# A Fourier-operator tokenizer with transformer: the mixing of modes without GpSimd and in a fixed order, its weights in eighths, its modes loaded in two parts

## The chip, the cores and the metric

One core of a Trainium2 chip. The metric is device time in microseconds (us). Engines are named as in the profile: PE multiplies matrices (PEld loads its weights), DVE, ACT and POOL (GpSimd) are the vector, scalar and general engines, SP only issues DMAs. A "q" behind a name (SPq, ACTq) is the engine's queue of DMA issues.

## What is computed

64 images of 256 x 256 pass a four-layer Fourier neural operator with 32 channels; its output, one value a pixel, is 256 rows of 256 values. With 77 text rows these are 333 tokens of 256, which pass one transformer layer (attention, and a feed-forward part for the 165 kept tokens). Cut to the part around the change:

```python
v = h @ p_w + p_b                                   # 3 -> 32 channels
for i in range(4):
    x_ft = rfft2(v)                                 # 24 x 12 modes are kept
    out_ft[:12, :12]  = einsum('bixy,ioxy->boxy', x_ft[:, :, :12, :12],  W1[i])
    out_ft[-12:, :12] = einsum('bixy,ioxy->boxy', x_ft[:, :, -12:, :12], W2[i])
    v = irfft2(out_ft) + einsum('bcxy,cd->bdxy', v, w_w[i]) + w_b[i]
    v = batchnorm(v)                                # over all images and pixels
    if i < 3: v = relu(v)
out = einsum('bcxy,cu->bxyu', v, q_w) + q_b         # then attention and feed-forward
```

All of it is in float32. The batch norm needs sums over all images before any pixel of the next layer can be made; the kernel takes them in the space of modes.

## The kernel before, in words

For each of the four layers there is a **mixing**, and after each of the first three a **pass** over the 64 images. The fourth mixing is followed by the transformer (`image_rows` to `feed_forward`).

A pass (`layer`) reads an image's pixels (tile vin, L578), makes the new pixels (`pre`: L614 from the mixed modes, L625 from the old pixels), applies ReLU into vo (L632 on ACT, L633 on DVE), stores vo (L634 on SP), transposes it into t32 (L637), squares a product for the variance (`product`, L649 and L656), and transforms the new pixels to modes: `along_y` (L666, four t32 tiles of an image, result zt by L676) and `along_x` (L689), whose 72 KB for one image (xo) are stored to xh_d in HBM (L697). `load_am` (L564) loads the mixed modes of an image, `scale_am` (L584, POOL) scales them into one of two tiles ams, `spread` (L595) is the first matmul with them. The pass is written in a region with manual schedule: each engine keeps the order in which the code is written. All else is ordered by the framework's scheduler, which simulates the program and issues what is ready by the order of writing.

A mixing has these steps. `mix_weights` makes the tiles wm of the two halves of mode rows from the weights in HBM: `piece(m)`, four pieces, loads 2.36 MB into a tile wn by four DMAs (L361; on SP in layer 0, on POOL in the others), then copies into wm (L376 and L378 on ACT, L380 on DVE); the first piece of a half also fills two slots on POOL (L366, L367). There is one wn tile in layer 0 and two in the others. L746 loads the modes of all 64 images, 4.7 MB, into the tile xh (in layer 0 `forward_first` makes them on the chip, with 12 additions at L302). `squares` sums the squares of the pass. `mix` then has 12 steps kp: 96 small matmuls (L412), an eviction into e by ACT (L424), four copies into the output tiles ob (L429 and L432 on DVE, L430 on POOL, L431 on ACT), two instructions and a product for the sums (L434, L438 or L440), their addition into acc (L441, POOL), copies for the edges (L442, L449), and four stores of 256 KB to mix_d (L451). There are three ob tiles of each part. After the 12 steps come the statistics (L458 to L486). `layer` begins with the constant rows of the two ams tiles: a memset (L536) and small DMAs on ACT's queue (L544), 28 in layer 0 and 4 in layers 1 and 2, and in layer 0 with two loads of 2 MB into the tiles mv (L557).

The pools of tiles are stacks of SBUF addresses: the pools of a pass lie where those of a mixing lay before, and the other way round. With `reuse_waits="tile"` a new tile waits only for the earlier tiles whose bytes it takes. In order of address, behind the constants (offsets in bytes of one partition, from the sizes in the code):

| | mixing, layers 1 to 3 | pass before |
|---|---|---|
| | wn 0, xh 36864, wm 73728 to 129024 | li (vin, mv) 0, lc (ams, sk) 32768, lt (t32) 39552, ly (y_) 121472, lo (vo) 137856, lz (zt) 170624, lx (xo) 178816, la (am) 179968 |

Of the kernel before, what the change touches and what calls it, by code (L numbers as in the profile page):

```python
# [9 lines left out]
F32 = mybir.dt.float32  # L10
# [7 lines left out]
C = 32  # L18
# [16 lines left out]
def _tables():  # L35
# [10 lines left out]
    def halves(a):  # L46
        return a.reshape(2, 128, -1).transpose(1, 0, 2)
# [34 lines left out]
    out["ones"] = np.ones((128, 128))  # L82
    out["chan"] = p[:, None] % C == np.arange(C)[None, :]

    out["fyr"] = halves(fy)
    out["fyi"] = halves(np.concatenate([np.sin(th), np.cos(th), np.zeros((S, 8))], 1))
    out["fxn"] = halves(np.concatenate([cs, grid[:, None], np.zeros((S, 15))], 1))
# [42 lines left out]
def tile_fno_fusion_transformer(ctx: ExitStack, tc: tile.TileContext, a, cst_d, grid_d, out):  # L130
# [14 lines left out]
        nc.sync.dma_start(t, cst_d[:, lo:hi])  # L145
        return lambda k: t[:, _AT[k][0] - lo:_AT[k][0] - lo + _AT[k][1]]

    tab = tables(const, "fyt", "chan", "cst")
    FYT = tab("fyt").rearrange("p (y k) -> p y k", y=8)
    EXL = {n: tab("ex" + n) for n in "EO"}  # L150
    FXL = {n: tab("fx" + n).rearrange("p (h k) -> p h k", h=2) for n in "EO"}
    T4, ID, ONES, CHAN = tab("t4"), tab("ident"), tab("ones"), tab("chan")

    epsc = const.tile([128, 1], F32, name="epsc")
    nc.vector.memset(epsc, EPS)
# [33 lines left out]
    def forward_first(xh, weights):  # L189
# [4 lines left out]
        with tc.tile_pool(name="f0", bufs=1) as fp, tc.tile_pool(name="f0i", bufs=3) as ip, \  # L194
# [42 lines left out]
                    )  # L237

            weights(0)

            pw, pb = a["L0_tok_p_w"], a["L0_tok_p_b"].rearrange("(o c) -> o c", o=1)
            pwR = fp.tile([128, C], F32, name="pwR")
# [48 lines left out]
            for kyg in range(3):  # L291
                for ri in range(2):
                    t2 = [pq.tile([128, 2, 512], F32, name="xps") for _ in range(2)]
                    for j in range(4):
                        nc.tensor.matmul(
                            t2[j // 2][:, j % 2, :kn * B],
                            lhsT=px[32 * j:32 * j + KX, kyg, ri].rearrange("p q c -> p (q c)"),
                            rhs=xm[32 * j:32 * j + KX], start=True, stop=True, skip_group_check=True,
                        )
                    for j in range(2):  # L300
                        k0 = 2 * kn * j
                        nc.vector.tensor_tensor(  # L302
                            xh[:, kyg, ri, k0:k0 + 2 * kn, :].rearrange("p (j k) b -> p j k b", j=2),
                            t2[j][:, :, :kn * B].rearrange("p j (k b) -> p j k b", b=B),
                            g[:, kyg, ri, k0:k0 + 2 * kn, :].rearrange("p (j k) o -> p j k o", j=2)
                            .to_broadcast([128, 2, kn, B]),
                            ALU.add,
                        )
                if kyg < 2:
                    weights(kyg + 1)  # L310
            weights(3)


            mo = fp.tile([128, 4], F32, name="mo")
# [34 lines left out]
    def mix_weights(i, wmp, wnp):  # L349

        wms = [wmp.tile([128, 3, M, 6, C], F32, name=f"wm{half}") for half in range(2)]

        def piece(m):
            half, oh = divmod(m, 2)
            wm, fw = wms[half], a[f"L0_tok_fw{half + 1}"]
            n = 16 * M * M * 2
            wn = wnp.tile([128, n], F32, name="wn")
            for k4 in range(4):  # L360
                (nc.gpsimd if i else nc.sync).dma_start(  # L361
                    wn[C * k4:C * k4 + C, 0:n - 2 * k4],
                    fw[i, :, 16 * oh:16 * oh + 16].rearrange("c o k l r -> c (o k l r)")[:, 2 * k4:],
                )
            if oh == 0:
                nc.gpsimd.memset(wm[:, :, :, 5, :], 0.0)  # L366
                nc.gpsimd.tensor_copy(  # L367
                    wm[:, :, :, 2, :].rearrange("p g k o -> p (g k) o"),
                    w4[i].rearrange("p (o c) -> p o c", o=1).to_broadcast([128, 3 * M, C]),
                )  # L370
            v = wn.rearrange("p (o k g q r) -> p g k o q r", o=16, k=M, g=3, q=4)
            for slot, ri in ((4, 1), (3, 0), (1, 0), (0, 1)):
                s_ = v[:, :, :, :, 0, ri]
                d_ = wm[:, :, :, slot, 16 * oh:16 * oh + 16]
                if slot == 0:
                    nc.scalar.mul(d_, s_, -1.0)  # L376
                elif slot == 1:
                    nc.scalar.copy(d_, s_)  # L378
                else:
                    nc.vector.tensor_copy(d_, s_)  # L380

        return wms, piece

    def mix(i, lhs, wm, u2):
# [5 lines left out]
        with tc.tile_pool(name="mo", bufs=1) as op, tc.tile_pool(name="me", bufs=3) as ep, \  # L390
                tc.tile_pool(name="mp", bufs=2, space=PSUM) as pp:
            NB = 3
            ob = [[op.tile([128, C, 32], F32, name=f"ob{p}_{n}") for n in range(NB)] for p in range(2)]
            for p in range(2):
                for n in range(NB):
                    nc.gpsimd.memset(ob[p][n], 0.0)
            acc = op.tile([128, 12, 2, C], F32, name="acc")
            f0 = op.tile([128, M, 2, C], F32, name="f0")
            fr = op.tile([128, M, 2, C], F32, name="fr")
# [3 lines left out]
            for kp in range(M):  # L403
                ps = pp.tile([128, 4, 512], F32, name="mps")
                wk, k0 = wm[2 * kp // M], 2 * kp % M
                for g in range(3):
# [11 lines left out]
                e = ep.tile([128, 3, 4, 4, C], F32, name="e")  # L418
                a_ = ep.tile([128, 12, 2, C], F32, name="a_")
                o0, o1 = (  # L420
                    ob[p][kp % NB][:, :, :KX].rearrange("p o (n k) -> p n k o", k=M) for p in range(2)
                )
                for hv in halves:
                    nc.scalar.copy(  # L424
                        e[hv].rearrange("p g q s o -> p q g (s o)"),
                        ps[hv, :, 0:384].rearrange("p q (g s) -> p q g s", g=3),
                    )
                    ev = e[hv].rearrange("p g q s o -> p (g q) s o")
                    nc.vector.tensor_copy(o0[hv, 0], ev[:, :, 1, :])  # L429
                    nc.gpsimd.tensor_copy(o0[hv, 1], ev[:, :, 2, :])  # L430
                    nc.scalar.mul(o1[hv, 0], ev[:, :, 2, :], -1.0)  # L431
                    nc.vector.tensor_copy(o1[hv, 1], ev[:, :, 1, :])  # L432
                    for n, (us, fs) in enumerate(((0, 1), (3, 2))):
                        nc.vector.scalar_tensor_tensor(  # L434
                            a_[hv, :, n, :], ev[:, :, us, :], 2.0, ev[:, :, fs, :], ALU.mult, ALU.add
                        )
                    if kp == 0:
                        nc.vector.tensor_mul(acc[hv], a_[hv], ev[:, :, 1:3, :])  # L438
                    else:
                        nc.vector.tensor_mul(a_[hv], a_[hv], ev[:, :, 1:3, :])  # L440
                        nc.gpsimd.tensor_add(acc[hv], acc[hv], a_[hv])  # L441
                    nc.scalar.copy(f0[hv, kp], ev[:, 0, 1:3, :])  # L442
                if kp == 0:
                    nc.vector.tensor_add(fin[0:B, 1, :], e[0:B, 0, 0, 1, :], e[0:B, 0, 0, 0, :])
                for kk in range(2):
                    to = (M - kp) % M if kk == 0 else M - 1 - kp
                    hv = slice(64 * kk, 64 * kk + B)
                    if kk or kp != M // 2:
                        nc.scalar.copy(fr[hv, to], e[hv, 0, 0, 1:3, :])  # L449
                    for p in range(2):  # L450
                        nc.sync.dma_start(  # L451
                            mix_d[i][:, p, 2 * kp + kk, :], ob[p][kp % NB][hv].rearrange("b o k -> b (o k)")
                        )
            for hv in halves:
                q = fin[hv, 0, :]
                t1 = op.tile([128, C], F32, name="t1", bufs=2)
# [45 lines left out]
    def layer(i, st, src, dst, acc):  # L502
# [7 lines left out]
        with ExitStack() as cx:  # L510
            def pool(name, bufs, **kw):
                return cx.enter_context(tc.tile_pool(name=name, bufs=bufs, **kw))

            ip = pool("li", 2 if i == 0 else 4, reuse_waits="tile")
            cp = pool("lc", 1, reuse_waits="tile")
            tp, yp, op, zp, xp = (
                pool(n, k, reuse_waits="tile") for n, k in (("lt", 5), ("ly", 2), ("lo", 4), ("lz", 1), ("lx", 2))
            )
            ap_ = pool("la", 2, reuse_waits="tile")
            pp = pool("lp", 4, space=PSUM)  # L520


            rv = cp.tile([128, 4, C], F32, name="rv")

            ams = [cp.tile([64 + rows_, 16 * C], F32, name=f"ams{n}") for n in range(2)]
            if i == 0:
                nc.vector.tensor_mul(rv[:, 0, :], s_, w0row[:, 3, :])
                nc.vector.tensor_add(rv[:, 0, :], rv[:, 0, :], t_)
# [3 lines left out]
            else:  # L532
                nc.vector.tensor_copy(rv[:, 0, :], t_)
            nc.vector.tensor_scalar_mul(rv[:, 0, :], rv[:, 0, :], float(S * S))
            for t in ams:
                nc.vector.memset(t, 0.0)  # L536
                av = t.rearrange("p (c k) -> p c k", k=32)
                halves = [(n, 64 * n, slice(16 * n, 16 * n + 16)) for n in range(2)]
                where = [(0, 48, 0)]
                if i == 0:  # L540
                    where += [(1, 48, 28), (2, 49, 0)] + [(3, 50 + j, 24 + j) for j in range(4)]
                for n, r, k in where:
                    for _, p0, cs in halves:
                        nc.scalar.dma_start(av[p0 + r:p0 + r + 1, :, k], rv[0:1, n, cs])  # L544
            sk = cp.tile([128, 16, 32], F32, name="sk")
            for _, p0, cs in halves:
                nc.vector.tensor_copy(
# [183 lines left out]
    st = None  # L731
    acc = None
    for i in range(L):
        with tc.tile_pool(name="wn", bufs=2 if i else 1, reuse_waits="tile") as wnp, \
                tc.tile_pool(name="xh", bufs=1, reuse_waits="tile") as xp, \
                tc.tile_pool(name="wm", bufs=1, reuse_waits="tile") as wmp:
            wm, piece = mix_weights(i, wmp, wnp)
# [3 lines left out]
                lhs = lambda band, g, ri, k: xh[band, g, ri, k, :]  # L741
            else:
                xh = xp.tile([128, B, 3, 2, KX], F32, name="xh")
                piece(0)
                piece(1)
                nc.sync.dma_start(xh.rearrange("p b g r k -> p b (g r k)"), xh_d[i - 1])  # L746
                u2 = squares(i, acc)
                piece(2)
                piece(3)
                lhs = lambda band, g, ri, k: xh[band, :, g, ri, k]  # L750
            st = mix(i, lhs, wm, u2)
        if i < L - 1:
            acc = const.tile([128, 16 * B], F32, name="acc") if acc is None else acc
            with tc.manual_schedule():
# [375 lines left out]
```

## Time and profile before

| | us |
|---|---|
| median of 3 runs | 12465.9 (12437.0 to 12485.34) |
| the profiled execution | 12478.4, span 12476.6 |
| PE busy | 11172.7 (90% of the span) |
| DVE, ACT, POOL busy | 8784.2, 6065.1, 1529.5 |
| mean clock granted to PE | 0.957 |
| from the first weight load of a mixing to the first matmul after it | 59.3 to 248.2; 3106.1 to 3257.1; 6403.0 to 6554.6; 9691.9 to 9857.9 |

In the lines below a row of a timeline has the start in us, the duration in us, the engine, the line of the code, the operation, output<-input with partitions x elements, how many instructions are merged, and in brackets how long the engine had stood still and what ended that. A row of windows has the window and its length, then for PE, PEld, DVE, ACT and POOL the busy us (and the number of instructions), then the granted clock (1.00 is full), the mean share in which the 16 DMA engines were busy, and GB/s.

### The profile page before, as it was taken

To read this page: it belongs to the slowest core of one execution; us is meant where nothing else is said; L and a number is where in the kernel's file an instruction comes from. 1 tells how busy PE (TensorE), PEld (TensorE's weight loads), DVE (VectorE), ACT (ScalarE), POOL (GpSimd) and SP (SyncE) were. 2 spreads that over 40 slices of the span, in tenths; PEclk is the share of its full clock that TensorE was granted. 3 is DMA by queue.
4 is the path that set the end of the run, shared out by engine and by line. 5 is a ranking of instruction groups with operands and counts; after the bars stand their busy time and mean duration, and the time that the engine had idled before them with its cause. 6 is when DMAs were issued, how large, how long until landed. Compare 5 with 4: busy or idle time off the path is not lost. (4 is left out here: it accounts for less than half of the span.)

```text
span 12476.6 us, 405217 instructions
## 1 busy us (share of the span) xinstructions
PE 11172.7 (90%) x182038; PEld 5874.2 (47%) x182038; DVE 8784.2 (70%) x10531; ACT 6065.1 (49%) x10217; POOL 1529.5 (12%) x2040
## 2 busy tenths in 40 slices
PE   4999999999699999999969999999999599999999
PEld 2444444444344444444434444444444366666666
DVE  4777777777677777777767776777777566666665
ACT  4555555555455555555545555555555333333333
POOL 1000000000100000000010000000000233333333
PEclk7999999999799999999989999999999799999999
DMA  6555555555899899889889898899899755555553
GB/s 187 199 202 202 201 202 202 200 201 203 286 350 350 346 351 353 344 345 349 341 277 358 345 354 347 341 351 352 345 352 352 255 218 229 232 227 221 221 231 151
DMA packets 588469, 3485.04 MB, mean 279 GB/s; under 512 B 96616, under 2 KB 146152, under 8 KB 189800
## 3 DMA queue, kind: packets, MB, share of 16 engines
q1 hardware_dynamic: 540288, 3405.18, 70.9%
q0 software_dynamic: 38144, 50.22, 1.8%
q8 instruction: 1423, 23.31, 0.7%
q10 hardware_dynamic: 8296, 3.72, 0.1%
q14 instruction: 318, 2.61, 0.1%
HBM read 1761.83 MB, written 1696.92 MB: 277 GB/s over the span
## 5 line engine op out<-in xcount | busy, mean ns | idle before, releaser
L656 ACT ACTIVATE ring<-ring 128x1024 f32<-128x1024 f32 x3072 | 3108.8, 1012 | 1185.5 <-PE ring L649 1148.6
L637 DVE STREAM_TRANSPOSE t<-vo 128x2048 f32<-128x2048 f32 x1536 | 3550.1, 2311 | 175.2 <-ACT vo L632 13.5
L649 PE MATMUL ring<-vo,w 32*32 32x512 f32 x49152 | 2851.0, 625 | 385.4 <-DVE zt L676 134.1
L632 ACT ACTIVATE vo<-ring 128x1024 f32<-128x1024 f32 x1536 | 1568.1, 1021 | 3045.8 <-PE ring L625 2386.1
L633 DVE TENSOR_SCALAR vo<-ring 128x1024 f32<-128x1024 f32 x1536 | 1858.6, 1210 | 615.0 <-PE ring L625 420.5
L666 PE MATMUL ring<-t,cst 32*32 32x512 f32 x49152 | 1867.6, 603 | 297.8 <-issue 296.6
L676 DVE STREAM_TRANSPOSE zt<-ring 128x1024 f32<-128x1024 f32 x384 | 712.3, 1926 | 1646.6 <-PE ring L666 1646.6
L649 PEld LDWEIGHTS ring<-vo,w 32*32 32x32 f32 x49152 | 765.5, 105 | 1886.4 <-ACT ring L656 473.7
L584 POOL TENSOR_TENSOR ams<-am,sk 48x512 f32<-48x512 f32 x384 | 486.7, 1268 | 8538.7 <-DMA am<-mix 8218.2
L666 PEld LDWEIGHTS ring<-t,cst 32*32 32x32 f32 x49152 | 976.3, 103 | 1145.6 <-issue 688.7
L625 PE MATMUL ring<-vin,ws 32*32 32x512 f32 x32768 | 1241.9, 607 | 21.2 <-issue 19.2
L689 PEld LDWEIGHTS ring<-cst,zt 128*128 128x128 f32 x4608 | 536.1, 194 | 179.4 <-ACT vo L632 159.5
L1079 POOL DMA_DIRECT2D out_dram<-o x1024 | 512.3, 509 | 660.1 <-DVE o L1074 628.8
L656 ACT ACTIVATION_READ_ACCUMULATOR ring<-ring 128x1 f32 x3072 | 584.2, 190 | 0.0
L689 PE MATMUL ring<-cst,zt 128*128 128x96 f32 x4608 | 568.3, 280 | 8.3 <-DVE zt L676 8.3
L878 PE MATMUL hp<-ch,win 128*32 128x512 f32 x4096 | 473.3, 602 | 8.6 <-DMA ch<-v 8.5
L595 PE MATMUL ring<-ams,cst 49*128 49x512 f32 (+1 forms) x1536 | 391.5, 620 | 99.4 <-POOL ams L584 88.7
L625 PEld LDWEIGHTS ring<-vin,ws 32*32 32x32 f32 x32768 | 253.8, 103 | 410.0 <-issue 382.8
L883 ACT ACTIVATE h<-hp,hbias 128x512 f32<-128x512 f32 x64 | 44.0, 687 | 597.5 <-PE hp L878 581.4
L412 PE MATMUL mps<-wm,xh 32*64 32x128 f32 (+1 forms) x4608 | 110.4, 354 | 242.2 <-DMA xh<-xh 110.8
L595 PEld LDWEIGHTS ring<-ams,cst 49*128 49x128 f32 (+1 forms) x1536 | 147.5, 188 | 349.8 <-issue 242.1
L1041 PE MATMUL pp<-zs,w 128*128 128x165 f32 x2048 | 302.4, 305 | 0.0
(932 smaller groups left out, 12039.4 us busy)
## 6 DMA issues: line engine op xcount, KB each, us to landing
v<-vo SPq DMA_DIRECT2D x1536, 1024.0 KB
vin<-v SPq DMA_DIRECT2D x1024, 1024.0 KB
ch<-v SPq DMA_DIRECT2D x512, 1024.0 KB
mix<-ob SPq DMA_DIRECT2D x192, 256.0 KB
am<-mix SPq DMA_DIRECT2D x384, 96.0 KB
xin<-in_x_dram SPq DMA_DIRECT2D x16, 1024.0 KB
mv<-in_x_dram SPq DMA_DIRECT2D x256, 64.0 KB
out_dram<-o POOLq DMA_DIRECT2D x1024, 16.0 KB, 3.0
```

The costliest lines, as they stand in the source:

```text
L584: nc.gpsimd.tensor_tensor(ams[b % 2][hv], a_[hv], sk[hv].rearrange("p c k -> p (c k)"), ALU.mult)
L595: nc.tensor.matmul(ps[:, n, :], lhsT=EX[hv, 128 * h:128 * h + 128], rhs=ams[b % 2][hv], start=True, stop=True, skip_group_check=True,)
L625: nc.tensor.matmul(ps[n][32 * j:32 * j + 32], lhsT=ws[32 * n:32 * n + 32], rhs=v[32 * n:32 * n + 32, 2 * j:2 * j + 2, :], start=False, sto ...
L632: nc.scalar.activation(of[:, 0:2], t2[0], AF.Relu)
L633: nc.vector.tensor_scalar(of[:, 2:4], t2[1], 0.0, None, ALU.max)
L637: nc.vector.transpose(t32[b, t // 2][:, :, 8 * (t % 2):8 * (t % 2) + 8, :].rearrange("p y s c -> p s y c"), o.rearrange("p s (y l) -> p s ...
L649: nc.tensor.matmul(ps[n][32 * j:32 * j + 32], lhsT=w4[i + 1][32 * n:32 * n + 32], rhs=o[32 * n:32 * n + 32, 2 * j:2 * j + 2, :], start=Tru ...
L656: nc.scalar.activation(t2[n], t2[n], AF.Square, accum_out=acc[:, at:at + 1])
L666: nc.tensor.matmul(ps[n][32 * j:32 * j + 32], lhsT=FYT[32 * n:32 * n + 32, k, :], rhs=t32[b, j][32 * n:32 * n + 32, k].rearrange("p s c -> ...
L676: nc.vector.transpose(zt[:, h].rearrange("p k c -> p c k"), t2[h].rearrange("p n (s c) -> p c (n s)", c=C),)
L689: nc.tensor.matmul(ps[:, 0, 96 * g:96 * g + 96], lhsT=zt[:, h, k0:k0 + 4, :].rearrange("p k c -> p (k c)"), rhs=FX[:, h, 48 * r:48 * r + 9 ...
L1079: nc.gpsimd.dma_start(out[b, 64 * n + 16 * g:64 * n + 16 * g + 16].rearrange("(p t) d -> p t d", t=2), o[32 * g + 8 * n:32 * g + 8 * n + 8 ...
```

## The change

1. Weights come in eight pieces of half the size, with two wn tiles in layer 0 and four in the others. In layer 0 two pieces are asked for before the parameters, the others two by two after each group of modes.
2. In layers 1 to 3 the modes are loaded in two parts: those of the first 56 images on POOL's queue, written after the first four pieces, those of the last eight on SP.
3. `mix` is put into a region with manual schedule. In it POOL's copy and addition go to DVE, one DVE copy goes to ACT and one ACT copy (f0) to DVE, and the copies into ob are written before the sums. The two parts of ob lie in one tile, so that a step has two stores of 512 KB.
4. The constant rows of ams come from a table of zeros and ones (64 KB more in the table of constants), multiplied by the row's values on DVE, without DMAs.
5. The pools of a pass have another order: lo 32768, ly 65536, la 81920, lc 86016, lx 93056, lz 94208, lt 102400 to 184320 (in bytes behind the constants, as above).

```diff
@@ forward_first
             weights(0)
+            weights(1)
...
-                if kyg < 2:
-                    weights(kyg + 1)
-            weights(3)
+                weights(2 * kyg + 2)
+                weights(2 * kyg + 3)
@@ mix_weights
-            half, oh = divmod(m, 2)
+            half, oh = divmod(m, 4)
...
-            n = 16 * M * M * 2
+            n = 8 * M * M * 2
@@ mix
-            ob = [[op.tile([128, C, 32], F32, name=f"ob{p}_{n}") for n in range(NB)] for p in range(2)]
-            for p in range(2):
-                for n in range(NB):
-                    nc.gpsimd.memset(ob[p][n], 0.0)
+            ob = [op.tile([128, 2, C, 32], F32, name=f"ob{n}") for n in range(NB)]
+            for t in ob:
+                nc.gpsimd.memset(t, 0.0)
...
+                    nc.scalar.mul(o1[hv, 0], ev[:, :, 2, :], -1.0)
+                    nc.scalar.copy(o1[hv, 1], ev[:, :, 1, :])
                     nc.vector.tensor_copy(o0[hv, 0], ev[:, :, 1, :])
-                    nc.gpsimd.tensor_copy(o0[hv, 1], ev[:, :, 2, :])
-                    nc.scalar.mul(o1[hv, 0], ev[:, :, 2, :], -1.0)
-                    nc.vector.tensor_copy(o1[hv, 1], ev[:, :, 1, :])
+                    nc.vector.tensor_copy(o0[hv, 1], ev[:, :, 2, :])
+                    nc.vector.tensor_copy(f0[hv, kp], ev[:, 0, 1:3, :])
...
-                        nc.gpsimd.tensor_add(acc[hv], acc[hv], a_[hv])
-                    nc.scalar.copy(f0[hv, kp], ev[:, 0, 1:3, :])
+                        nc.vector.tensor_add(acc[hv], acc[hv], a_[hv])
...
-                    for p in range(2):
-                        nc.sync.dma_start(
-                            mix_d[i][:, p, 2 * kp + kk, :], ob[p][kp % NB][hv].rearrange("b o k -> b (o k)")
-                        )
+                    nc.sync.dma_start(
+                        mix_d[i][:, :, 2 * kp + kk, :], ob[kp % NB][hv].rearrange("b p o k -> b p (o k)")
+                    )
@@ layer
-            for t in ams:
-                nc.vector.memset(t, 0.0)
...
-                        nc.scalar.dma_start(av[p0 + r:p0 + r + 1, :, k], rv[0:1, n, cs])
...
+            for n in range(nr):
+                nc.vector.tensor_tensor(
+                    a1 if n else a0, rh[:, n].to_broadcast([128, 16, 32]),
+                    CROW[:, n:n + 1, :].to_broadcast([128, 16, 32]), ALU.mult,
+                )
+                if n:
+                    nc.vector.tensor_add(a0, a0, a1)
+            nc.vector.tensor_copy(ams[1], ams[0])
@@ the loop over the layers
-        with tc.tile_pool(name="wn", bufs=2 if i else 1, reuse_waits="tile") as wnp, \
+        with tc.tile_pool(name="wn", bufs=4 if i else 2, reuse_waits="tile") as wnp, \
...
-                piece(0)
-                piece(1)
-                nc.sync.dma_start(xh.rearrange("p b g r k -> p b (g r k)"), xh_d[i - 1])
+                early = max(B - 8, 0)
+                for m in range(4):
+                    piece(m)
+                if early:
+                    nc.gpsimd.dma_start(
+                        xh[:, :early].rearrange("p b g r k -> p b (g r k)"), xh_d[i - 1][:, :early]
+                    )
+                nc.sync.dma_start(
+                    xh[:, early:].rearrange("p b g r k -> p b (g r k)"), xh_d[i - 1][:, early:]
+                )
                 u2 = squares(i, acc)
-                piece(2)
-                piece(3)
+                for m in range(4, 8):
+                    piece(m)
...
-            st = mix(i, lhs, wm, u2)
+            with tc.manual_schedule():
+                st = mix(i, lhs, wm, u2)
```

## The prediction

> **What bounds the kernel now.** I first read the page's rows of 40 slices: PE is at 9 tenths nearly everywhere, with a dip at each of the four mixings. Inside the passes (3300 to 6300 us) PE is busy 2771 of 3000 us and the clock granted is 0.99; the change touches nothing there. So I read the four gaps, from the first weight load of a mixing to the first matmul after it: 59.3 to 248.2 us (layer 0), 3106.1 to 3257.1, 6403.0 to 6554.6, and 9691.9 to 9857.9. The middle two are alike. The view of windows for the second (span, then PE, PEld, DVE, ACT, POOL, clock, DMA share, GB/s):
>
> ```profile
> 3106.00:3152.00 46.00, 19.25 (x346) 11.08 (x342) 14.91 (x14) 10.86 (x16) 17.68 (x26) 0.72 1.01 241
> 3152.00:3166.00 14.00, 0.00 (x0) 0.00 (x0) 0.00 (x0) 0.00 (x0) 0.00 (x0) 0.50 0.97 354
> 3166.00:3188.00 22.00, 10.65 (x480) 9.92 (x480) 15.25 (x20) 13.74 (x20) 7.39 (x5) 0.73 0.02 6
> 3188.00:3224.00 36.00, 17.44 (x672) 15.81 (x672) 32.78 (x37) 21.45 (x38) 20.79 (x14) 0.55 0.90 243
> 3224.00:3244.00 20.00, 0.66 (x2) 0.50 (x2) 16.18 (x37) 3.69 (x8) 5.32 (x5) 0.50 0.37 84
> ```
>
> The DMA engines are full until 3166, then empty for 22 us, full again, and mostly empty for 20 us before the end. No compute engine is full throughout. The timeline of SP's queue and then of PE says why:
>
> ```profile
> 3130.73 0.32 SPq L697 DMA_DIRECT2D xh<-xo  x1
> 3145.97 0.32 SPq L746 DMA_DIRECT2D xh<-xh  x1
> 3187.51 63.10 SPq L451 DMA_DIRECT2D mix<-ob  x48
> 3253.61 0.79 SPq L564 DMA_DIRECT2D am<-mix  x2
> ```
>
> ```profile
> 3168.52 7.59 PE L412 MATMUL mps<-wm,xh 32*64 32x128 f32 x326 [37.36 <-DMA xh<-xh]
> ...
> 3257.13 5.11 PE L595 MATMUL ring<-ams,cst 49*128 49x512 f32 x8 [21.07 <-POOL ams L584]
> ```
>
> The one load of all modes (L746) stands until the pass's last 72 KB store (L697) has landed, 14.8 us by SP's waits, and the mixing until that load has landed. Its first store leaves only at 3187.5, since the scheduler put the copies into ob behind the sums and the weights of the second half. The last stores leave after the statistics, and the load of am waits for them. DVE's timeline shows the second fault:
>
> ```profile
> 3177.58 2.67 DVE L434 SCALAR_TENSOR_TENSOR a__30837<-e 128x384 f32<-128x384 f32 x2
> ...
> 3186.57 0.48 DVE L429 COPY ob<-e 128x384 f32<-128x384 f32 x1
> ...
> 3188.96 1.03 DVE L434 SCALAR_TENSOR_TENSOR a__30904<-e 128x384 f32<-128x384 f32 x2 [0.93 <-ACT e L424]
> ...
> 3195.16 2.12 DVE L432 COPY ob<-e 128x384 f32<-128x384 f32 x1
> ```
>
> The same pair of L434 takes 1.03 us while POOL is idle and 2.67 while POOL adds (L441 at 3177.75); a copy 0.48 or 2.12. Layer 0, by windows and by ACT's timeline:
>
> ```profile
> 76.00:100.00 24.00, 13.40 (x66) 7.47 (x62) 17.77 (x38) 2.71 (x3) 4.72 (x6) 0.62 0.05 12
> 100.00:112.00 12.00, 0.00 (x0) 0.00 (x0) 0.16 (x1) 0.18 (x1) 0.69 (x1) 0.50 0.83 173
> ...
> 200.00:230.00 30.00, 0.66 (x2) 0.50 (x2) 6.45 (x29) 2.02 (x3) 0.00 (x0) 0.50 0.43 96
> 230.00:248.00 18.00, 0.00 (x0) 0.00 (x0) 0.00 (x0) 0.00 (x0) 1.09 (x1) 0.50 0.73 255
> ```
>
> ```profile
> 206.22 6.92 ACTq L544 DMA_DIRECT2D ams<-rv  x11
> 213.18 0.85 ACT L431 ACTIVATE ob<-e 128x384 f32<-128x384 f32 x1 [6.13 <-DMA ams<-rv]
> 213.21 13.54 ACTq L544 DMA_DIRECT2D ams<-rv  x16
> ```
>
> With one weight buffer the DMA engines stand idle from 76 to 100, and 28 tiny DMAs on ACT's queue hold up the last copies into ob, behind them the last stores, the 4 MB of mv and am.
>
> **The floor.** I price a gap by what the DMA engines must move, as they are its fullest resource. Weights: 9.43 MB, queue q0 used 21.2% of 195 us in the window 3085 to 3280, so 41.3 us. Modes: 4.72 MB at 354/0.97 = 365 GB/s, 12.9. Stores of mix: 12.58 MB at 243/0.90 = 270 GB/s, 46.6. The pass's last v stores: some 4. Sum 105 us from 3106.1, so 3211; the ends (last store to am to POOL to PE, 3250.3 to 3257.1) add 6.8: 3218, against 3257.1. So 39 us of this gap are DMA idleness.
>
> **The change, part by part, in gaps 2 and 3.**
> *Modes of 56 images early.* By the order of the pools the modes' tile now lies on the vo tiles and one y_ tile, free after the last transpose and store of vo, about 3112, no longer on t32 (free after along_y, 3122). 4.13 MB move under along_y and along_x; 0.59 MB stay behind L697. The load goes to POOL's queue, in order behind 16 weight issues of 0.49 us; it adds one issue. The price of the new places: wm's first half now lies on xo and zt, so its copies wait until the last xo store lands. Before, they ran at 3122.4. I keep 14.8 us for that store (3145.5), and five us of copies after it: the first matmul at about 3152, not 3168.5. Behind that wait stand POOL's memset and copy (2.2 us) and, if the scheduler puts them first, POOL's later loads, so between 3135 (store lands at once) and 3158 (early load behind the memset); I take 3152.
> *Weights in eighths.* Same bytes. 32 issues for 16, 7.8 us more on POOL, hidden as POOL has no arithmetic left. 16 more copies, each with a fixed 0.19 us by ACT's rows (64 elements 0.24, 1536 1.44): 1.6 us on ACT and on DVE, inside the coupling below. But pieces 4 to 7 can load only after pieces 0 to 3 are copied, now about 3149: some 20 us of DMA that lay before 3152 move beside the stores. The sum of bytes holds that already.
> *No GpSimd, fixed order.* DVE per step: two copies 0.49, the f0 copy about 0.15 (nearest row L442 on ACT, 0.25), the pair 1.03, product 0.96, the add that was L441 0.96 (row L440): 4.1 us, 49 for 12, plus 4.6 for the weights' copies. ACT: 1.44 + 0.88 + 0.88 + 0.49 = 3.7. POOL's 1.1 and 1.8 us and their slowing of DVE go. PE's 96 matmuls take 2.6. Stores need 46.6/12 = 3.9 us a step. A new wait: in fixed order o1 on ACT and o0 on DVE wait until the store of three steps before has landed, and the next eviction and the sums stand behind them. First eviction 3155, so DVE is done by 3210; the statistics take 5.8 + 0.8 + 2.3 us by their rows, constants 2.7: 3222, POOL and PE 3223.
> *Constant rows.* In layers 1 and 2 four DMAs of 0.6 us on ACT go; three to four DVE instructions of 0.5 replace two memsets of 0.49: within 1 us. The table is 64 KB more at the start: 0.2 us.
> DMA path 3218, engine path 3223, nearly level. For their coupling (stores beside weights, a drained queue about 3147) I add 6: 3229. Gain **28** each.
>
> **Layer 0.** xin's rest 4, weights 9.43 MB at 173/0.83 = 208 GB/s 45.3, stores 46.6, mv 4.19 MB 10.5 (387 GB/s at share 0.97), ends 9.7: 59.3 + 116 = 175, against 248.2. Kept idle: some 12 us while the first copies of weights wait in DVE's order for the 12 adds of L302 (77.7 to 88.4), and 10 of coupling: 198. The constants cost about 5 us of DVE for 1.0 of memsets, under mv's load; without that cover 4 us. Gain **50**.
> **Layer 3.** Weights, modes, stores 100.8, v 3, the transformer's parameters 13 (ACT's queue, 7.8% of 166 us) and tables 2: 119; ends 12.9: 9824 against 9857.9. The parameter issues stay on ACT between the mixing's steps (they held L431 5.2 and 4.7 us), now in a fixed chain: I keep 14. Gain **20**.
> Sum 50 + 28 + 28 + 20 = **126 us**. The profiled execution took 12478.4 (span 12476.6): it would take 12352. The median of the three is 12.5 lower: 12340.
>
> **Two rules of the skill.** The Trainium skill, SBUF — State Buffer, section "SBUF: two separate sides", speaks against this change: descriptors of POOL's DMAs can't be written while DVE copies fp32 in SBUF, and the summary says to issue from SP or ACT. Its example goes from 620 to 3100 ns. Row: L361, 489 ns in median, 712 at most, six of 16 while DVE was busy 9.7 of 10 us (in transposes, not copies). By the row nothing; by the rule 16 pieces beside the mixing would each land up to 2.5 us late, 40 us if in series, under 22 us of loads that must run anyway: 10 to 20 a gap. I take the row and keep the rule for the range. DMA: Bandwidth & Descriptors, "Queues, rings and completion order", says that an engine takes queues in turn by packets; the 72 KB would then land in about 2 us and the start come at 3142. The row says 14.8. It is worth at most 6 us, as the stores end last.
>
> **Rivals.**
> A, chance 0.62: as worked out, 12340.
> B, 0.12: all idleness goes except layer 0's 12 us and 4 a gap: 60 + 35 + 35 + 30 = 160, 12306. For it: the slack is real; against: copies must wait for loads.
> C, 0.12: the stores starve behind the eighths as L697 did, ob's wait then stops ACT and DVE until the loads end, about 3180, and all 46.6 us follow: 3180 + 46.6 + 6.8 = 3233 plus coupling 4. Gains 33, 20, 20, 12 = 85: 12381.
> D, 0.10: the scheduler, outside the fixed part, sets loads and copies as late as before; the start stays at 3168 and only the tail's idleness goes (13 us of the 20): 35 + 14 + 14 + 7 = 70, 12396; one part of this is a change that doesn't do what it says.
> E, slower, 0.04: the pools' new order puts vin, vo and t32 elsewhere; should a pass run slower by that, in its 9.2 ms (three passes), 1.4% eats the 126, and from 2.1% it is slower by over 0.5%: at 2.5% 12340 + 230 = 12570. Against it: same instructions, tiles, buffers and queues; no row shows a cost by place.
> A measurement here tells 0.5% (62 us) from no change. Faster: A, B, most of C, six tenths of D: 0.90; within 0.5%: 0.07; slower 0.03. The range 12295 to 12402 takes A to D with the bounds above; E and the worst of D are left out.
>
> **What would show it.** L412's first matmul near 3152 in gap 2 and under 106 in layer 0; a load xh<-xh on POOL before along_y's end; L451 spread evenly over 45 to 60 us from 3 us after the first eviction, no DMA hole over 8 us after it; pairs of L434 at 1.0 always; no L544. The passes must keep their length to 0.2%, else E. Holes of 15 us with ob's wait on ACT mean C; the old start means D.

## The result and the profile after

The changed kernel takes 12362.4 us (median of 4 runs, 12360.6 to 12374.6) where the kernel before takes 12468.7 on the same chip (4 runs): ratio 0.992, 95% interval 0.9899 to 0.9941. The profiled execution has a span of 12358.8 us against 12476.6, 117.8 less.

To place these 117.8 us I cut both spans at the same points. A gap now runs from the pass's last group of L699 (L689 before; line numbers rise by about 10) to the first matmul after the mixing; layer 0's from the span's start to its first ring matmul. Before: 248.2, 132.8, 134.4, 145.8 us. After: 191.2, 109.9, 109.5, 134.6. That is 57.0 + 22.9 + 24.9 + 11.2 = 116.0; the three passes and the transformer together went from 11815.4 to 11813.6. The gain is in the gaps. (The medians differ by 106.3: the kernel before was profiled in one of its longer executions, 12478.4 us.)

The second gap after, in the view of windows:

```profile
3048.00:3070.00 22.00, 16.98 (x312) 10.57 (x282) 7.13 (x7) 4.02 (x9) 0.95 (x2) 0.84 0.46 141
...
3093.00:3105.00 12.00, 6.46 (x287) 6.28 (x272) 1.94 (x4) 3.45 (x5) 3.93 (x9) 0.64 1.02 219
3105.00:3117.00 12.00, 0.30 (x7) 0.01 (x2) 4.82 (x10) 5.28 (x11) 5.35 (x4) 0.50 0.61 131
3117.00:3158.00 41.00, 23.58 (x864) 20.21 (x864) 39.98 (x79) 37.00 (x54) 0.00 (x0) 0.62 0.97 284
```

From 3117 on it is what was meant: DVE busy 39.98 of 41 us, ACT 37.00, the DMA engines full. But ahead of that PE stands (0.30 of 12 us) while DVE and ACT are half idle, and at the end of the pass the DMA engines are half empty (0.46), though the early load was to run there. The timelines of POOL, of SP's queue and of ACT show both:

```profile
3045.58 3.37 POOL L369 DMA_DIRECT2D wn<-in_L_tok_fw_dram  x7 [38.85 <-PE ring L624]
3071.03 1.06 POOL L374 MEMSET wm<- 128x1152 f32 x1 [22.08 <-DMA xh<-xo]
...
3075.62 0.55 POOL L758 DMA_DIRECT2D xh<-xh  x1
...
3092.58 0.49 POOL L369 DMA_DIRECT2D wn<-in_L_tok_fw_dram  x1 [9.43 <-DMA xh<-xh]
```

```profile
3069.18 0.32 SPq L707 DMA_DIRECT2D xh<-xo  x1
3070.93 0.32 SPq L761 DMA_DIRECT2D xh<-xh  x1
3116.57 9.20 SPq L457 DMA_DIRECT2D mix<-ob  x6
```

```profile
3095.19 1.44 ACT L431 COPY e<-mps 128x1536 f32<-128x1536 f32 x1 [11.39 <-PE mps L419]
...
3104.31 0.71 ACT L386 COPY wm<-wn 128x288 f32<-128x288 f32 x1 [5.16 <-DMA wn<-in_L_tok_fw_dram]
...
3109.74 0.72 ACT L386 COPY wm<-wn 128x288 f32<-128x288 f32 x1 [4.10 <-DMA wn<-in_L_tok_fw_dram]
...
3110.98 0.86 ACT L436 ACTIVATE ob<-e 128x384 f32<-128x384 f32 x1
3114.42 0.71 ACT L386 COPY wm<-wn 128x288 f32<-128x288 f32 x1 [2.58 <-DMA wn<-in_L_tok_fw_dram]
3115.03 0.71 ACT L384 ACTIVATE wm<-wn 128x288 f32<-128x288 f32 x1
3115.64 0.87 ACT L437 COPY ob<-e 128x384 f32<-128x384 f32 x1
```

POOL stands 22 us at the memset of wm, which now lies on xo and waits for xo's last store, and the "early" load of the modes leaves 4.7 us after the late one. The first eviction (3095.2) is followed by its copies into ob only at 3111 and 3115.6: on ACT (and alike on DVE) the copies of pieces 4 to 7 stand ahead of them and wait for their loads. Nine of the 16 issues of these loads leave POOL only from 3092.6 on. By the trace's semaphores (111 to 118, used in turn) every DMA of POOL's queue waits until the eighth before it has landed, and for the one at 3092.58 that was the load of the modes. The first store leaves 24 us after the first matmul; before the change it was 19.

### The profile page after: what moved, and what is told of

It reads as the page before. It is cut to its first block, busy times and chain, and to the rows that moved or that the text cites. A ratio compares the mean times of both kernels' runs of the same rounds, so it can differ in the third digit from the quotient of the medians.

```text
span 12358.8 us, 405064 instructions
## 1 busy us (share of the span) xinstructions
PE 11164.5 (90%) x182038; PEld 5874.0 (48%) x182038; DVE 8774.8 (71%) x10667; ACT 6094.5 (49%) x10249; POOL 1412.7 (11%) x1987
## 5 line engine op out<-in xcount | busy, mean ns | idle before, releaser
L699 PEld LDWEIGHTS ring<-cst,zt 128*128 128x128 f32 x4608 | 536.4, 194 | 174.6 <-ACT vo L642 161.6
L699 PE MATMUL ring<-cst,zt 128*128 128x96 f32 x4608 | 568.7, 281 | 8.1 <-DVE zt L686 8.1
L605 PE MATMUL ring<-ams,cst 49*128 49x512 f32 (+1 forms) x1536 | 391.5, 621 | 37.6 <-POOL ams L594 27.2
L1070 PE MATMUL pp<-g,w 128*128 128x165 f32 x2048 | 298.6, 303 | 0.0
```

The lines of the kernel that those rows point to most:

```text
L699: nc.tensor.matmul(ps[:, 0, 96 * g:96 * g + 96], lhsT=zt[:, h, k0:k0 + 4, :].rearrange("p k c -> p (k c)"), rhs=FX[:, h, 48 * r:48 * r + 9 ...
L1070: nc.tensor.matmul(ps[:, :KEPT], lhsT=w2[:, hb, 128 * dh:128 * dh + 128], rhs=g[:, hb, :], start=hb == 0, stop=hb == HID // 128 - 1,)
```

## The experiments

Passes and transformer together vary between 11798 and 11831 us from one profile to another, in no order that follows a kernel's edit; so the verdicts rest on the gaps of one profile each, which repeat within a microsecond or two where an edit doesn't touch them. By the times alone, only the intervals of u_order, m_best and m_top3 lie clear of that of after. u_ kernels undo one part of the changed kernel, b_ does two parts alone in the kernel before, m_ changes it further.

| kernel | time, us | gap 1 | gap 2 | gap 3 | gap 4 | ratio to before, 95% |
|---|---|---|---|---|---|---|
| before | 12468.7 | 248.2 | 132.8 | 134.4 | 145.8 | |
| after | 12362.4 | 191.2 | 109.9 | 109.5 | 134.6 | 0.9899 to 0.9941 |
| u_modes | 12368.5 | 190.2 | 110.4 | 110.0 | 137.5 | 0.9904 to 0.9933 |
| u_order | 12416.1 | 211.1 | 117.3 | 120.0 | 140.6 | 0.9942 to 0.9971 |
| u_gps | 12386.5 | 194.3 | 118.4 | 120.1 | 133.1 | 0.9919 to 0.9949 |
| u_eighths | 12373.0 | 203.3 | 110.7 | 110.4 | 133.4 | 0.9909 to 0.9942 |
| u_pools | 12345.3 | 193.3 | 101.7 | 102.8 | 126.2 | 0.9873 to 0.9906 |
| u_const | 12388.6 | 204.2 | 109.6 | 109.2 | 133.0 | 0.9917 to 0.9947 |
| u_pm | 12363.5 | 190.2 | 109.7 | 108.3 | 132.6 | 0.9901 to 0.9934 |
| b_nogps | 12397.5 | 221.0 | 111.7 | 110.6 | 130.4 | 0.9930 to 0.9959 |
| m_late | 12340.9 | 189.2 | 102.2 | 103.2 | 121.9 | 0.9883 to 0.9912 |
| m_best | 12315.4 | 185.3 | 97.4 | 97.2 | 112.4 | 0.9860 to 0.9890 |
| m_top | 12324.2 | 186.3 | 98.5 | 101.7 | 118.9 | 0.9870 to 0.9899 |
| m_top3 | 12317.6 | 180.6 | 98.8 | 102.2 | 118.5 | 0.9860 to 0.9893 |

My theory after reading the trace: fixed order and GpSimd's absence make the gain, and the stall at pieces 4 to 7 gives back what the earlier start brings. The rival is the one on record: the earlier start (modes and eighths) and the stores beside the loads make it.

**u_modes: all modes in one load on SP.**

```
-                early = max(B - 8, 0)
+                early = 0
```

> The changed kernel with all 64 images' modes in the one load on SP behind the last store of xo; nothing else is undone. If the load of 56 images on POOL is what brought the start forward, the 4.13 MB (11.3 us at 365 GB/s) come back behind that store: gaps 2 to 4 each some 8 to 11 us longer, 12362 + 30 = 12392 us. If, as the trace of after suggests, that load leaves only behind POOL's memset of wm (3075.6, later than the store has landed, 3070.9), nothing is lost: gap 2 within 3 us of 109.9 (last L699 group to first L605), 12362 +- 8 us.

Gaps 2 and 3 grew by 0.5 us, gap 4 by 2.9. In the changed kernel the early load is worth next to nothing.

**u_order: the mixing left to the scheduler.**

```
-            with tc.manual_schedule():
-                st = mix(i, lhs, wm, u2)
+            st = mix(i, lhs, wm, u2)
```

> The changed kernel without the fixed order: the mixing is left to the scheduler, still without GpSimd. If the fixed order is what spread the stores, the copies into ob slip behind the sums again as before, the last stores leave after the statistics: each of four gaps 8 to 12 us longer, 12362 + 40 = 12402 us. If the stall between the first two evictions (13 us, where both engines stand at weight copies of the second half) is made by that order, the free order fills it: each gap up to 10 us shorter, 12325. No matter: 12362 +- 8.

The gaps grew by 19.9, 7.4, 10.5 and 6.0 us, 44 in all. In gap 2 the stores are spread over 54 us and the last leaves 9 us after the statistics' matmul; in the changed kernel it leaves 7 us ahead of it. SP's queue of u_order:

```profile
3138.71 54.08 SPq L457 DMA_DIRECT2D mix<-ob  x24
```

So the order does what the diff says; but the stall was there without it too (first store at 54.6 us from the group, 54.0 with it): the copies of the pieces stand ahead in either case.

**u_gps: one copy and the add back on GpSimd.**

```
-                    nc.vector.tensor_copy(o0[hv, 1], ev[:, :, 2, :])
+                    nc.gpsimd.tensor_copy(o0[hv, 1], ev[:, :, 2, :])
...
-                        nc.vector.tensor_add(acc[hv], acc[hv], a_[hv])
+                        nc.gpsimd.tensor_add(acc[hv], acc[hv], a_[hv])
```

> The changed kernel, fixed order kept, with one copy into ob and the add of the sum given back to GpSimd, as before. If GpSimd's access slows DVE as in the trace of before (pair of L434 2.67 against 1.03 us), the step of the mixing goes from 3.66 us to about 4.6: 12 steps, 11 us a gap, 12362 + 40 = 12402 us. If the relief of DVE (1.45 us less a step) and the slowing cancel, the step stays at ACT's 3.6: 12362 +- 8.

Gaps 2 and 3 grew by 8.5 and 10.6 us, gap 1 by 3.1, gap 4 not (-1.5). A DVE step took 4.5 us instead of 3.7, though DVE has two operations less. First DVE's timeline of the changed kernel, then that of u_gps, one step each in part:

```profile
3119.11 0.20 DVE L440 COPY f<-e 128x64 f32<-128x64 f32 x1
3119.19 1.02 DVE L442 SCALAR_TENSOR_TENSOR a__30791<-e 128x384 f32<-128x384 f32 x2
```

```profile
3141.76 1.78 DVE L440 COPY f<-e 128x64 f32<-128x64 f32 x1
3143.46 1.62 DVE L442 SCALAR_TENSOR_TENSOR a__31051<-e 128x384 f32<-128x384 f32 x2
```

The 64-element copy into f0 takes 1.78 us while POOL adds (1.83 us from 3141.65), and 0.20 alone. What slows is whichever DVE instruction falls beside POOL's, as the row of before said. Over the four mixings of u_gps this copy takes 0.18 to 0.21 us alone, 0.87 to 1.01 beside POOL's copy (1.1 to 1.25 us) and 1.74 to 1.79 beside its addition. In gap 4 it falls beside the addition in two steps of twelve, in the other gaps in seven to nine; that fits the gap that didn't grow, but isn't shown to be its cause.

**u_eighths: weights in quarters, two buffers, one in layer 0.**

```
-            half, oh = divmod(m, 4)
+            half, oh = divmod(m, 2)
...
-        with tc.tile_pool(name="wn", bufs=4 if i else 2, reuse_waits="tile") as wnp, \
+        with tc.tile_pool(name="wn", bufs=2 if i else 1, reuse_waits="tile") as wnp, \
```

> The changed kernel with the weights in quarters and 2 buffers (1 in layer 0), as before. If the second buffer in layer 0 brought its gain, layer 0's first mixing matmul slips from 107 to about 114 and its gap by some 25 to 45 us; gaps 2 to 4 within 5 us each (same bytes, half the pieces): 12362 + 40 = 12402 us. If layer 0's gain came from the fixed order and the constants instead, its gap stays within 8 us: 12370.

Gap 1 grew by 12.1 us (first matmul 113.8 for 107.3), between the two expectations; gaps 2 to 4 by 0.8, 0.9 and -1.2. The eighths, with the second buffer, pay in layer 0 alone.

**u_pools: the passes' pools in the order of before.**

```
-            op, yp, ap_, cp, xp, zp, tp = (
...
+            cp = pool("lc", 1, reuse_waits="tile")
+            tp, yp, op, zp, xp = (
```

> The changed kernel with the passes' pools in the order of before, so that wm, wn and the modes' tile lie where they lay. The first matmul of gap 2 came 29.9 us after the pass's last L699 group, against 44.1 before, and neither the early load nor the eighths made that (31 to 33 and 29 us without them). If the order of the pools did (wm's copies and POOL's memset now stand until xo has landed, the POOL queue runs dry, so xo's 72 KB land in 1.8 us and not 14.8), the start goes back to 40 to 44 and gaps 2 to 4 grow by 8 to 12 us each: 12362 + 30 = 12392. If the fixed order of the mixing made it, by another order of POOL's queue, nothing changes: 12362 +- 8.

Both expectations were wrong: gaps 2 to 4 became 8.2, 6.7 and 8.4 us *shorter*. SP's queue and POOL of u_pools (its last group at 3070.9):

```profile
3077.47 0.32 SPq L708 DMA_DIRECT2D xh<-xo  x1
3091.26 0.32 SPq L762 DMA_DIRECT2D xh<-xh  x1
3116.82 41.37 SPq L457 DMA_DIRECT2D mix<-ob  x24
```

```profile
3073.50 0.55 POOL L759 DMA_DIRECT2D xh<-xh  x1
```

With wm not on xo, POOL's memset waits for nothing of the pass's end, the early load leaves 2.6 us after the group (13.0 in the changed kernel), and the loads of the weights run on. The price is the one the prediction named: xo's store lands after 13.8 us and not 1.8, as it shares the engines with POOL's loads. The start is later (33.6 for 29.9 us), the first store is earlier (45.9 for 54.0).

**u_pm: the same, without the early load.** The edits of u_pools and u_modes together.

> The kernel with the pools of before (u_pools, 12345 us) and, besides, without the early load: all 64 images in one load on SP. In u_pools the early load left 2.6 us after the last L699 group, ahead of xo's last store; here the whole 4.72 MB stand until that store has landed (20.4 us after the group). If the early load is worth something once it is early, the first matmul slips from 33.6 to 41 to 45 us and gaps 2 to 4 grow by 6 to 9 us each: 12345 + 22 = 12367. If the eight late images and the weights' copies set the start anyway: 12345 +- 8.

First matmul at 43.5 us, gaps 8.0, 5.5 and 6.4 us longer than u_pools. With u_modes and the changed kernel this makes a square for gap 2: new pools 109.9 with the early load and 110.4 without; old pools 101.7 and 109.7. Early load and old pools are worth 8.7 us together, and apart 0.5 and 0.7. In gap 3 it is 7.2 together, 0.5 and 1.7 apart; in gap 4 11.3 together, 2.9 and 4.9 apart. Also: u_pm starts 14 us later than the changed kernel, and its first store leaves at the same 53.95 us after the group. In gap 2 the earlier start of the changed kernel is worth nothing.

**b_nogps: the kernel before with the fixed order and without GpSimd.**

```
+            with tc.manual_schedule():
+                st = mix(i, lhs, wm, u2)
...
-                    nc.gpsimd.tensor_copy(o0[hv, 1], ev[:, :, 2, :])
+                    nc.vector.tensor_copy(o0[hv, 1], ev[:, :, 2, :])
...
-                        nc.gpsimd.tensor_add(acc[hv], acc[hv], a_[hv])
+                        nc.vector.tensor_add(acc[hv], acc[hv], a_[hv])
```

> The kernel before with two parts of the change alone: the mixing in a fixed order, and GpSimd's copy and add given to DVE (quarters, pools, load of the modes and constants as before). Undone one at a time from the changed kernel these two were worth 44 and 21 us of the four gaps. If they stand by themselves: 12469 - 65 = 12404. If most of it needs the earlier loads (the order then also fixes ACT and DVE behind the copies of quarters 2 and 3, whose loads end late): half, 12437, or none.

72 of the 106 us, near the first expectation. (The code of before has the copies into ob ahead of the sums already; the fixed order keeps them there.) Gaps 2 and 3 are 111.7 and 110.6, within 2 us of the whole change, and gap 4 is 4 us better than it. Here the quarters have landed when the mixing starts: the copies of the second half stand ahead of ob's as well, but wait for nothing (ACT of b_nogps):

```profile
3144.10 1.23 ACT L378 COPY wm<-wn 128x576 f32<-128x576 f32 x1
...
3148.62 0.86 ACT L431 ACTIVATE ob<-e 128x384 f32<-128x384 f32 x1
```

In layer 0 this gives 27.2 of 57.0; the eighths (12.1) and the constants (below) hold most of the rest.

**u_const: constant rows by DMAs from ACT's queue again.**

```
-                nc.vector.tensor_tensor(
-                    a1 if n else a0, rh[:, n].to_broadcast([128, 16, 32]),
...
+                        nc.scalar.dma_start(av[p0 + r:p0 + r + 1, :, k], rv[0:1, n, cs])
```

> The changed kernel with the constant rows written by small DMAs from ACT's queue, as before (28 in layer 0, 4 in layers 1 and 2). If ACT's issues count on the path: 28 x 0.6 = 17 us after rv is ready (180.5), plus 2 to land, against 6.6 us on DVE: layer 0's gap 8 to 12 us longer, layers 1 and 2 by 0 to 2: 12362 + 12 = 12374. If the load of mv and am (to 189) hides them: 12362 +- 6.

Gap 1 grew by 13.0 us, gaps 2 to 4 by -0.3, -0.3, -1.6. ACT's timeline in layer 0, then a row of SP's waits there (us in total, times, longest):

```profile
180.61 20.47 ACTq L549 DMA_DIRECT2D ams<-rv  x28
```

```profile
SPq L562 <- DMA ams<-rv: 18.0, 1, 18.0
```

28 issues take 20.5 us, and the trace puts a wait of SP's second load of mv down to them; am's load follows only at 200.6 (174.4 in the changed kernel). The code doesn't say why that load should wait for them, but the trace's semaphores do. The DMAs of SP and ACT together set eight of them (100 and 102 to 108), each when it lands, and wait until theirs is free. The load waits for 100, which ACT's DMA of 190.22 sets ahead of it; am's load, behind it, waits for five more of the eight. The time grew by 26 us, 15 more than the gaps, and in all four runs (12382.6 to 12393.3); this profile's passes are among the longest (17 us over the changed kernel's), which I can't tie to the edit.

**m_late: copies of pieces 4 to 7 inside the fixed order.**

```
+            late = [load(m) for m in range(4, 8)]
...
+                if 1 <= kp <= 4:
+                    conv(3 + kp, late[kp - 1])
```

Here `load` and `conv` are the two halves of `piece`; in layer 0 these four loads go to POOL's queue.

> The changed kernel with the loads and copies of the weights' second half (pieces 4 to 7) written inside the fixed order, one piece's copies after each of steps 1 to 4, and in layer 0 their loads on POOL's queue, no longer ahead of the stores on SP's. If the stall between the first two evictions (ACT and DVE stand at copies of pieces 4 to 7 that wait for loads, 13 us in each gap) is on the path, the first store of gap 2 leaves at about 37 us after the last L699 group and not at 54, 12 steps of 3.7 and four pieces of 1.3 us end at about 85, the gap is 100 us and not 110; layer 0 some 10 us shorter: 12362 - 40 = 12322. If the DMA engines are the bound (only 4.7 us of their idleness lie in that stall), some 5 us a gap: 12342. If stores starve beside the loads and ob's wait stops ACT: no gain, 12362.

SP's queue of m_late in gap 2 (its last group at 3054.3):

```profile
3089.77 53.08 SPq L467 DMA_DIRECT2D mix<-ob  x24
```

The first store of gap 2 leaves at 35.5 us, the gap falls by 7.7, gap 3 by 6.3, gap 4 by 12.7, layer 0 by 2.0. The stall was on the path; of its 18.5 us some 11 are given back: the stores now run beside those loads, and their issues span 53 us, 42 in the changed kernel.

**m_best: m_late, and all early loads ahead of POOL's memset.**

```
+                wns = [load(0), load(1)]
...
+                wns += [load(2), load(3)]
+                for m in range(4):
+                    conv(m, wns[m])
```

The load of 56 images stands at the line between; the memset and the copy of w4 move into `conv`.

> m_late, and in layers 1 to 3 POOL's queue takes all loads of pieces 0 to 3 and the modes of 56 images ahead of the memset of wm that waits for the last store of xo: the loads run in the 22 us in which POOL stood (DMA share 0.46 there, 12 us idle). If that idleness is what the early load was to use, the first matmul comes at about 20 us after the last L699 group (not 29.9) and the gap is some 8 to 12 us shorter than m_late's: 3 x 10 off m_late, 12362 - 40 - 30 = 12292. If the 72 KB of xo then land late again behind POOL's loads (14.8 us as before), the start stays at 28 to 31 and the time that of m_late.

Gaps 97.4, 97.2 and 112.4, the shortest of all; 12315 us, 47 less than the changed kernel. Windows of m_best:

```profile
3036.00:3062.00 26.00, 22.07 (x392) 11.97 (x388) 12.67 (x9) 8.80 (x17) 5.87 (x12) 0.91 0.84 295
3062.00:3079.00 17.00, 0.79 (x10) 0.69 (x18) 5.81 (x11) 5.39 (x9) 5.77 (x5) 0.50 0.82 214
...
3085.00:3140.00 55.00, 22.12 (x913) 19.78 (x901) 46.23 (x87) 41.65 (x63) 7.28 (x12) 0.68 0.99 288
```

The DMA engines are 0.84 busy before the pass ends and 0.99 through the stores. Against m_late gaps 2 to 4 lost 4.8, 6.0 and 9.5 us, about two thirds of what I expected: xo's store landed after 11.3 us.

**m_top: m_best with the pools of before.** The edit of u_pools.

> m_best with the pools in the order of before. If wm's place on xo costs the same 8 us a gap here as in the changed kernel (u_pools), gaps 2 to 4 go from 97.4, 97.2 and 112.4 to about 89, 89 and 104: 12315 - 24 = 12291. If m_best's early loads have taken that gain already, and xo's 72 KB land late again (20 us after the group and not 18, 17 and 15), the start stays at 22 to 26 us: 12315 +- 8.

Gaps 1.1, 4.5 and 6.5 us longer than m_best's: the first expectation was wrong, and the time lies just above the second. What u_pools gained was the early loads' way past the memset, and m_best has that already. With the old places its early load leaves later: 1.8, 1.4 and 1.7 us ahead of the group, for 3.3, 9.8 and 11.9.

**m_top3: parameters on POOL's queue, three weight buffers in layer 0.**

```
-    nc.scalar.dma_start(w1, a["L0_ffn_w1"].rearrange("(h p) f -> p h f", p=128))
+    nc.gpsimd.dma_start(w1, a["L0_ffn_w1"].rearrange("(h p) f -> p h f", p=128))
...
-        with tc.tile_pool(name="wn", bufs=4 if i else 2, reuse_waits="tile") as wnp, \
+        with tc.tile_pool(name="wn", bufs=4 if i else 3, reuse_waits="tile") as wnp, \
```

> m_top with the transformer's parameters issued on POOL's queue, no longer on ACT's between the steps of the mixing (gap 4), and three weight buffers for two in layer 0 (gap 1). If ACT's held issues are on gap 4's path (L431 waited 4.1 and 3.0 us behind them, L436 up to 7 us), gap 4 falls by 8 to 12 us against m_top; if the DMA engines bound it (0.93 full over its stores), by under 3. In layer 0 the first matmul moves from 107 to about 100 if the loads of pieces 0 to 3 set it (DMA share 0.59 before it), and its gap falls by up to 7; else 0. In sum m_top - 14, or m_top +- 5.

Gap 4 stayed (118.5 for 118.9): by this pair ACT's issues cost nothing there. Layer 0's first matmul came at 101.2 for 107.0, its gap fell by 5.7. m_best with three buffers in layer 0 would, by the gaps, be some 6 us below 12315; it wasn't run.

## Why the prediction held, and where its steps failed

The predicted 12340 is 22 us off, inside the range; the gain was 106 and not 126. By gaps: 57, 23, 25, 11 for a predicted 50, 28, 28, 20. Part of this is luck: layer 0's 7 us above the forecast cover two fifths of the 17 that the other gaps lack. In gap 2, counted from the last group (the prediction's times less 3124.4):

| step | predicted | measured |
|---|---|---|
| early load of the modes leaves | -12 | 13.0 |
| xo's last store lands after | 14.8 us | 1.8 us |
| first matmul | 27.6 | 29.9 |
| from the first eviction to DVE's last sum | 49 + 4.6, + 6 for coupling | 64.1 (gap 3) |
| statistics, constants, POOL | 12.6 | 13.1 (gap 3) |
| end of the gap | 104.6 | 109.9 |

- **The start** was right for a wrong pair of reasons. The early load went out behind POOL's memset, the case that I had as a bound (3158); and because POOL stood, xo's store had the engines to itself and landed at once. The two errors cancel, by luck.
- **What the start is worth**: this step failed. I counted 16.5 us of earlier start as gain, and said of pieces 4 to 7 that the sum of bytes holds them already. Bytes don't say in which order ACT and DVE take their work: the copies of these pieces stand ahead of the first copies into ob, wait 5.2, 4.1 and 2.6 us on ACT for loads, of which POOL issued nine of 16 only from 3092.6 on, after a wait of 9.4 us for the modes, and the first store leaves where it left with a start 14 us later (u_pm): 20 us after the end of the first eviction, for the 3 that I had named as a sign. "Coupling", set at 6 us, was some 15: 64.1 less twelve steps of 3.7 and 5.0 us of DVE's copies of weights. m_late, with these copies after steps 1 to 4, takes 6 to 13 us off each of gaps 2 to 4.
- **Fixed order and GpSimd**: right, and better than priced. A step took 3.7 us for my 4.1 on DVE, and the stores moved at 284/0.97 = 293 GB/s, 3.6 us a step for my 3.9. Why they moved faster is open: my row was of stores alone too (the last weights had landed at 3162.9), and the same quotient is 253/0.89 = 284 in b_nogps with stores of 256 KB and 242/0.96 = 252 in u_gps with stores of 512. That repaid part of the stall. Pairs of L442 take 1.01 to 1.06 us in gap 2. b_nogps shows that these two parts make 21.1 of the 22.9 us in gap 2 and 23.8 of 24.9 in gap 3, while the new order of the pools costs 7 to 8 us a gap (u_pools).
- **Layer 0**: 50 against 57. The undone parts give order 20, constants 13, eighths 12, GpSimd 3, and 9 that only show together. The wait that I kept (copies behind the adds of L311, 12 us) is there as a wait for loads: ACT waited 11.7 and 13.9 us for wn, and a third buffer took 6 us off.
- **Layer 3**: 20 against 11. I kept 14 us for parameter issues held on ACT. The view of waits on ACT in gap 4's stores (9655 to 9714; us in total, times, longest) has them:

```profile
ACT ob L436 <- DMA mix<-ob: 11.8, 3, 7.1
ACT e L431 <- issue: 7.1, 2, 4.1
```

  but with the issues on POOL's queue the gap is the same (m_top3 beside m_top), so it isn't ACT. What was mis-sized is the same stall as in gap 2: m_late takes 12.7 us off here. The rest isn't shown; the parameters' 13 us of DMA run beside the stores, whose 24 issues span 59 us, 42 in gap 2.
- **Constants** within 1 us in layers 1 and 2: right (-0.3). In layer 0 their DVE work (180.7 to 187.2) lies under am's load, which POOL waits for until 189.9, as said.
- **Rivals**: E didn't happen (passes and transformer 1.8 us shorter in 11815). B and C neither: ob's wait cost ACT 11.8 us in gap 4 and next to nothing in gap 3 (0.16). D was right in what it named, that the scheduler sets the loads and copies; only it set the copies early and the load late.
- **The skill's two rules**: the Trainium skill, SBUF — State Buffer, "SBUF: two separate sides", would have POOL's DMA issues starve beside DVE's copies. In the changed kernel 17 of 96 issues of L369 fall beside such copies; the median of all is 489 ns and the longest 696, so the row was right for it. It isn't right for every kernel: in m_best eight of 13 issues that fall beside DVE's copies into ob take 0.82 to 1.22 us. That is up to 0.7 us more, not the 2.5 that I had by the rule.
- The same skill, DMA: Bandwidth & Descriptors, "Queues, rings and completion order", has an engine take queues in turn by packets. The rule held; my 2 us for xo's 72 KB were wrong, since they left out how long the other queue's turn is. The trace of u_pools shows the turns. The store is 128 packets of 576 bytes, eight an engine if they are spread evenly. They run from 3081.7 to 3089.5, most of them 16 in every 1.2 us, and between the first and the last POOL's queue moves 118 packets, 91 of them of 32 KB: about one for each of the store's. With POOL's queue dry, in the changed kernel, the same 128 packets pass in 0.3 us.

## What to carry to other kernels

A sum of bytes can be reached only if each engine's order lets the transfers start: ask of every copy placed between two steps what it waits for, and what stands behind it on its engine. A tile's place in memory is a wait too: wm on xo stopped POOL's queue, and with it the load that the change was to bring forward. Undo parts in pairs as well as singly, since in gap 2 two parts were worth 8.7 us together and under 1 apart.

## What the runs showed that I had not expected

- A 64-element DVE copy that falls beside POOL's add takes 1.78 us and 0.20 alone; its time follows POOL's instruction (1.83 us), not its own size. In u_order one takes 3.50 us (3128.03 to 3131.53) beside POOL's memset of ob, which ends at 3131.47.
- The same 72 KB store lands in 1.8 us or in 11 to 14, by whether another queue's loads are under way: its small packets take turns with large ones.
- A few small DMAs can hold up a load on another engine's queue, since SP's and ACT's DMAs take the same eight semaphores in turn (u_const).
- SP's queue in layer 0 held the stores behind 32 issues of weights until 129.4 us, 18 us after the first eviction had ended; letting them go at 113.2 (m_late) gave only 2 us, though the DMA engines' share from 113 to 129 us went from 0.49 to 0.95: the stores then ran beside the loads.
